# Opening of a two-layer transformer kernel: norms in halves, one load of the first input, kept projections in half pieces

## The chip, the cores and the metric

The kernel runs on one core of one Trainium2 chip. Its five engines are TensorE (PE), VectorE (DVE), ScalarE (ACT), GpSimd (POOL) and SyncE (SP). The metric is the device time of one execution in microseconds (us), taken as the median of several runs.

## What is computed

Four sequences (b = 0 to 3) of 1024 tokens with 256 features go through two layers. Each layer is an attention and a feed-forward part, and after each part the input is added and the row is normalised. Only the first attention is touched by the change:

```python
qkv = jnp.einsum('bsc,oc->bso', x, w_qkv).reshape(B, S, 3, H, D)   # H = 16 heads, D = 16
q = layer_norm(qkv[:, :, 0], q_gamma, q_beta)                      # over the 16 elements of a head
k = layer_norm(qkv[:, :, 1], k_gamma, k_beta)
v = qkv[:, :, 2]
q, k = apply_rope(q, k)
attn = softmax(einsum('bqhd,bkhd->bhqk', q * D ** -0.5, k))
out = einsum('bhqk,bkhd->bqhd', attn, v).reshape(B, S, C) @ w_proj.T + b_proj
x = layernorm(x + out)
# then: gated feed-forward with integer weights; causal attention with a geometric term (8 heads);
# a mixture of 16 experts, two per token, with capacity 512; each followed by add and layernorm
```

All tensors are float32, apart from the three integer weights of the gated feed-forward.

## The kernel before

The first attention works on groups of four heads: a sequence has four groups (G0 = 4), and n = 4 * b + g numbers them. The order of instructions on every engine is written out by hand. Each engine runs its own list in order and waits on semaphores where it needs another's result; SP's list holds nearly all DMA issues.

**Projections.** The three weights (q, k, v) lie side by side in `w0`, 768 columns. The columns of q and k are centred over each head first, so that the mean in the norm falls away and only a sum of squares is left. A projection is cut into pieces j = 0 to 3 of 256 tokens. For each, `load_xin` loads a 256 KB tile of the transposed input (tag "xin", two buffers), four matmuls of 128x256 fill one PSUM bank, and ScalarE copies it out. `project_qk(b, pr)` does q and k for eight heads (pr is 0 or 1), with the sums of squares (`squares`, `sums`) and the inverse roots (`roots`); for b = 0, pr = 0 the root is taken at the end by ScalarE's Sqrt and VectorE's reciprocal, otherwise by GpSimd's power, 16 columns at a time. `project_v(b)` writes into `va0`, the one tile of values. `bank(name, big)` gives either one of six score banks (tag "s") or the single bank "m", which transposes use too.

**Stashes.** The projections of b = 1 to 3 don't fit into SBUF beside their turn. `stash_qk(b, pr)` and `stash_v(b)` compute them during the first batch and store them to DRAM (`qk_d`, `ss_d`, `v_d`); `load_heads` and `load_v` read them back. Only the values of b = 1 aren't kept: `project_v(1)` runs between the first two batches. The stored tile `xs` has one buffer, so the next stash's first copy waits until the store has read it.

**Maxima and attention.** `Maxima` turns the normalised heads (`rotate`: six steps for each of q and k and each half of the tokens), transposes them into `qT` and `kT` (`turn`), and computes the score matrix once only for the row maxima: `head(i, h)` is a matmul into a score bank and a VectorE reduction (tile `part`). `close` places the maxima into the 17th row of the query tile, so that the second computation of the scores has them subtracted. `Attend` computes the scores again, transposed (`sc`), exponentiates them on ScalarE (`pe`) and multiplies with the values (`av`).

**Order.** The opening projects for the first group and rotates it. Then come 16 units of maxima alone, group 0's: four maxima matmuls and four reductions each, with a projection piece of `early` beside most of them. `first_units(b)` then yields 64 units for a sequence: four scores, four maxima of the group after, one `av` of the unit before (four matmuls). `weave(units, n, pieces, ...)` spreads a list of pieces over the units, one piece after a unit, and runs `later` work at each `tick`; its `side` list adds one step of preparation to each unit (loads of x, `empty_slots`, weight conversion `dequant`). `empty_slots` fills the expert buffers `disp_d` in DRAM from a tile of zeros in twelve DMAs of 520 KB. In the first batch the pieces are 32 stashed ones and the mid step `load_heads(1, 0)` at unit 30.

Of the kernel before, what the change touches and what calls it, by code (L numbers as in the profile page):

```python
# [35 lines left out]
def postln_layers_kernel(ctx: ExitStack, tc: tile.TileContext, a: dict, out: bass.AP):  # L36
# [74 lines left out]
    with ExitStack() as main:  # L111
# [41 lines left out]
        for c in range(2):  # L153
            nc.sync.dma_start(w0[:, c], a["w0qkv"][c * P : (c + 1) * P, :])
# [10 lines left out]
        wsum0 = act.tile([P, 32], F32, tag="hT", bufs=1, name="wsum0")  # L165
        for c in range(2):
            w3 = w0[:, c, 0 : 2 * C].rearrange("p (h d) -> p h d", h=32)
            nc.vector.tensor_reduce(wsum0, w3, AX.X, ALU.add)
            nc.vector.tensor_scalar_mul(wsum0, wsum0, -1.0 / D0)
            nc.vector.tensor_tensor(w3, w3, wsum0.unsqueeze(2).to_broadcast([P, 32, D0]), ALU.add)  # L170
# [31 lines left out]
        nc.vector.memset(tokk, 0.0)  # L202
        nc.vector.memset(tokk[:, :, :, 16:17], 1.0)
        va0 = fa.tile([P, TB, H0, 32], F32, name="va0")
        nc.vector.memset(va0[:, :, :, 16:32], 1.0)
        nm3 = act.tile([P, 4, 4, 32], BF16, name="nm3")
        nc.vector.memset(nm3, 0.0)
# [4 lines left out]
        def project_qk(b, pr, first=False):  # L212


            def piece(j, big):
                if j == 0:
                    heads[b, pr] = (
                        fa.tile([P, TB, 2, 8, D0], F32, tag="xr", bufs=1, name=f"xr_{b}_{pr}"),
                        fa.tile([P, TB, 2, 8], F32, tag="ss", bufs=1, name=f"ss_{b}_{pr}"),
                    )  # L220
                xr, ss = heads[b, pr]
                xin = load_xin(b, j, f"k{pr}")
                ps = bank(f"qk0_{b}_{pr}_{j}", big)
                for i in range(2):
                    for c in range(2):
                        nc.tensor.matmul(
                            ps[:, i * 256 : (i + 1) * 256],
                            xin[:, c, i * P : (i + 1) * P],
                            w0[:, c, pr * 256 : (pr + 1) * 256],
                            start=c == 0,  # L230
                            stop=c == 1,
                        )
                x = xr[:, 2 * j : 2 * j + 2].rearrange("p t s h d -> p (t s h d)")
                nc.scalar.copy(x, ps)
                part = ss[:, 2 * j : 2 * j + 2].rearrange("p t s h -> p (t s h)")

                def squares():
                    sq = act.tile([P, 512], F32, tag="q1", bufs=G1, name=f"sq0_{b}_{pr}_{j}")
                    nc.gpsimd.tensor_tensor(sq, x, x, ALU.mult)

                    def sums():
                        nc.vector.tensor_reduce(part, sq.rearrange("p (h d) -> p h d", d=D0), AX.X, ALU.add)

                    return sums

                def roots(k):
                    p = part[:, 16 * k : 16 * k + 16]
                    if k == 0:
                        nc.gpsimd.tensor_scalar(part, part, D0 * 1e-6, None, ALU.add)
                    nc.gpsimd.tensor_tensor(p, p, neg_half.to_broadcast([P, 16]), ALU.pow)  # L250

                if first:
                    squares()()
                    if j == 3:
                        flat = ss.rearrange("p t s h -> p (t s h)")
                        nc.vector.tensor_scalar_add(flat, flat, D0 * 1e-6)
                        nc.scalar.activation(flat, flat, AF.Sqrt)
                        nc.vector.reciprocal(flat, flat)
                else:

                    def start():
                        sums = squares()
                        later(1, sums)

                    later(1, start)
                    for k in range(2):
                        later(3 + k, lambda k=k: roots(k))

            return [lambda big, j=j: piece(j, big) for j in range(4)]

        def project_v(b):
            def piece(j, big):
                xin = load_xin(b, j, "v")
# [21 lines left out]

        def stash_qk(b, pr):
            kept = {}

            def piece(j, big):
                if j == 0:  # L300
                    kept["x"] = act.tile([P, TB * 256], F32, tag="va1", bufs=1, name=f"xs_{b}_{pr}")
                    kept["ss"] = act.tile([P, TB * 16], F32, tag="k1", bufs=G1, name=f"sss_{b}_{pr}")
                xin = load_xin(b, j, f"k{pr}")
                ps = bank(f"qk0_{b}_{pr}_{j}", big)
                for i in range(2):
                    for c in range(2):
                        nc.tensor.matmul(  # L307
                            ps[:, i * 256 : (i + 1) * 256],
                            xin[:, c, i * P : (i + 1) * P],
                            w0[:, c, pr * 256 : (pr + 1) * 256],  # L310
                            start=c == 0,
                            stop=c == 1,
                        )
                x = kept["x"][:, j * 512 : (j + 1) * 512]
                nc.scalar.copy(x, ps)
# [15 lines left out]
            return [lambda big, j=j: piece(j, big) for j in range(4)]  # L331

        def stash_v(b):
            def piece(j, big):
                xin = load_xin(b, j, "v")
                ps = bank(f"v0_{b}_{j}", big)
                for i in range(2):
                    for c in range(2):
                        nc.tensor.matmul(
                            ps[:, i * 256 : (i + 1) * 256],  # L340
                            xin[:, c, i * P : (i + 1) * P],
                            w0[:, c, 512:768],
                            start=c == 0,
                            stop=c == 1,
                        )
                x = act.tile([P, 512], F32, tag="nmT", bufs=2, name=f"vs_{b}_{j}")
                nc.scalar.copy(x, ps)
                later(1, lambda: nc.sync.dma_start(v_d[b][:, j * 512 : (j + 1) * 512], x))

            return [lambda big, j=j: piece(j, big) for j in range(4)]  # L350
# [29 lines left out]
        class Maxima:  # L380


            def __init__(self, b, g, engines):
# [6 lines left out]

                def rotate(s, u):
                    eng, to_tok = engines[s], (self.tok, tokk)[s]
# [6 lines left out]
                    z = fa.tile([P, 4, 4, D0], F32, tag="tmpz", bufs=1, name=f"z0_{b}_{g}_{s}_{u}")  # L399
# [14 lines left out]
                def steps():  # L414
                    for s, u in ((0, 0), (1, 0), (0, 1), (1, 1)):
# [607 lines left out]
        both_pool = (nc.gpsimd, nc.gpsimd)  # L1023

        def first_units(b):
# [3 lines left out]
            for g in range(G0):  # L1029
# [3 lines left out]
                for i in range(16):  # L1033
# [27 lines left out]
                    if i == 3 and n + 2 < G0 * B:  # L1061
                        nb, ng = divmod(n + 2, G0)
                        groups[n + 2] = Maxima(nb, ng, both_pool)
# [84 lines left out]
        straight(project_qk(0, 0, first=True))  # L1148
        groups[0] = Maxima(0, 0, (nc.gpsimd, nc.vector))
        groups[0].rotate()  # L1150
        for k in range(4):
            groups[0].turn(k // 2, k % 2, big=k % 2 == 0)
        groups[1] = Maxima(0, 1, both_pool)

        b0p = wp.tile([P, C], F32, name="b0p")
        nc.scalar.dma_start(b0p, a["b0p"].partition_broadcast(P))
        w0p = wp.tile([P, 2, C], F32, name="w0p")
        nc.scalar.dma_start(w0p, a["w0p"].rearrange("(c p) f -> p c f", p=P))
# [400 lines left out]
```

## Time and profile before

| what | value |
|---|---|
| median of 3 runs | 2500.72 us (2499.29 to 2504.57) |
| profiled execution, its own time | 2496.14 us |
| span of the profiled execution | 2494.4 us |
| mean granted TensorE clock | 0.959 |
| PE busy | 2330.1 us |
| DVE busy | 1387.3 us |
| ACT busy | 1014.6 us |
| POOL busy | 769.8 us |
| 0 to 34.6 us (to the first reduction of maxima) | PE 15.71, DVE 21.26, ACT 7.56, POOL 21.11 us busy |
| 34.6 to 91.8 us (maxima of group 0 alone) | PE 50.99, DVE 44.17, ACT 11.29, POOL 38.73 us busy |
| 87.3 to 410 us (first batch) | PE 314.42, DVE 192.57, ACT 177.65, POOL 119.89 us busy |
| 410 to 430 us (between the batches) | PE 13.92, DVE 2.78, ACT 4.79, POOL 5.83 us busy |

The profile is of one execution; its times are us from the first instruction. A busy time counts instructions at work, not those that wait, and issues of DMAs don't count. The span leaves out what lies around the instructions, so the execution's own time is a little longer. "A <- B" in brackets says what ended an engine's idle time.

### The profile page before, as it was taken

To read this page: it belongs to the slowest core of one execution; us is meant where nothing else is said; L and a number is where in the kernel's file an instruction comes from. 1 tells how busy PE (TensorE), PEld (TensorE's weight loads), DVE (VectorE), ACT (ScalarE), POOL (GpSimd) and SP (SyncE) were. 2 spreads that over 40 slices of the span, in tenths; PEclk is the share of its full clock that TensorE was granted. 3 is DMA by queue.
4 is the path that set the end of the run, shared out by engine and by line. 5 is a ranking of instruction groups with operands and counts; after the bars stand their busy time and mean duration, and the time that the engine had idled before them with its cause. 6 is when DMAs were issued, how large, how long until landed. Compare 5 with 4: busy or idle time off the path is not lost.

```text
span 2494.4 us, 36151 instructions
## 1 busy us (share of the span) xinstructions
PE 2330.1 (93%) x14004; PEld 1162.9 (47%) x14004; DVE 1387.3 (56%) x3233; ACT 1014.6 (41%) x1995; POOL 769.8 (31%) x1111
## 2 busy tenths in 40 slices
PE   6999999999999999999989999999999974999994
PEld 4343344444444454444445434445556432666662
DVE  6765554766656747687565567825645774111113
ACT  1455454555453345545523455463332331111112
POOL 5723622524123313454042321211112145212223
PEclk8999999999998999999989999999999886999997
DMA  3134223000000000001000000102000012444444
GB/s 96 31 108 134 73 66 101 1 27 1 1 1 27 1 1 1 24 24 54 24 8 1 1 1 1 46 23 99 1 1 1 1 48 73 102 103 118 104 89 145
DMA packets 79772, 109.87 MB, mean 44 GB/s; under 512 B 8944, under 2 KB 68592, under 8 KB 77936
## 3 DMA queue, kind: packets, MB, share of 16 engines
q1 hardware_dynamic: 54080, 80.21, 9.9%
q0 software_dynamic: 9984, 14.82, 3.1%
q10 hardware_dynamic: 15536, 12.53, 1.7%
q8 instruction: 110, 1.80, 0.3%
q14 instruction: 62, 0.51, 0.1%
HBM read 68.64 MB, written 38.90 MB: 43 GB/s over the span
## 4 chain that ended last, share of the span: by engine, by line
PE 85%; DVE 8%; POOL 3%; DMA 2%; issue 1%; ACT 1%; ACTq 0%; SPq 0%; DVEq 0%; POOLq 0%
PE sc L468 19%; PE av L486 10%; PE ph L1420 7%; PE gu L632 7%; PE py L1436 7%; PE sc L958 5%; PE mx L444 5%; PE mx L908 4%; PE p L877 4%; PE dn L648 3%; PE av L995 3%; PE dn L995 2%; DVE masked L918 2%; PE ppa L566 2%; PE qk L307 2%; PE pt L435 1%
## 5 line engine op out<-in xcount | busy, mean ns | idle before, releaser
L447 DVE TENSOR_REDUCE part<-mx 128x1 f32<-128x512 f32 x1024 | 656.3, 684 | 353.5 <-PE mx L444 347.4
L477 ACT ACTIVATE pe<-sc 128x512 f32<-128x512 f32 x1024 | 554.1, 596 | 392.8 <-PE mx L444 332.9
L444 PE MATMUL mx<-kT,qT 32*128 32x512 f32 x2048 | 654.1, 645 | 5.5 <-DVE part L447 5.2
L468 PE MATMUL sc<-qT,kT 32*128 32x512 f32 x2048 | 620.5, 637 | 0.3 <-ACT pe L477 0.3
L468 PEld LDWEIGHTS sc<-qT,kT 32*128 32x128 f32 x2048 | 184.1, 183 | 227.3 <-issue 180.2
L486 PE MATMUL av<-pe,va 128*32 128x512 f32 x2048 | 273.6, 606 | 0.0
L969 ACT ACTIVATE pe<-sc 128x512 f32<-128x512 f32 (+3 forms) x384 | 157.5, 497 | 205.7 <-PE sc L958 199.1
L444 PEld LDWEIGHTS mx<-kT,qT 32*128 32x128 f32 x2048 | 198.9, 186 | 56.1 <-DVE part L447 29.6
L918 DVE CUSTOM_DVE_ANT_0 masked<-mx,mask_w 128x128 bf16<-128x128 f32 (+3 forms) x256 | 125.4, 490 | 111.7 <-PE mx L908 80.5
L1420 PE MATMUL ph<-dmT,f 128*128 128x512 f32 x384 | 169.5, 600 | 4.4 <-DVE dmT L99 3.5
L1436 PE MATMUL py<-f,hTm 128*128 128x256 f32 x768 | 167.7, 379 | 0.0
L1428 ACT ACTIVATE hTm<-ph,b 128x512 f32<-128x512 f32 x96 | 60.7, 683 | 260.6 <-PE ph L1420 260.6
L972 POOL TENSOR_SCALAR_AFFINE_SELECT pe<-pe 128x256 f32<-128x256 f32 x128 | 54.1, 432 | 363.0 <-ACT pe L969 361.5
L1440 POOL DMA_INDIRECT acc_d<-yo,dm x48 | 74.7, 1556 | 284.0 <-DVE yo L1438 233.9
L1436 PEld LDWEIGHTS py<-f,hTm 128*128 128x128 f32 x768 | 146.1, 190 | 24.8 <-issue 5.7
L908 PE MATMUL mx<-kT,qT 32*128 32x512 f32 (+3 forms) x768 | 138.0, 577 | 4.7 <-DVE x L533 3.6
L365 POOL TENSOR_TENSOR ss<-ss,neg_half 128x16 f32<-128x16 f32 x48 | 139.1, 2906 | 0.5
L1437 DVE TENSOR_TENSOR yo<-py,b 128x256 f32<-128x256 f32 x48 | 20.4, 425 | 206.7 <-PE py L1436 206.7
L958 PE MATMUL sc<-qT,kT 32*128 32x512 f32 (+3 forms) x768 | 131.5, 569 | 4.0 <-DVE part L918 2.2
L486 PEld LDWEIGHTS av<-pe,va 128*32 128x32 f32 x2048 | 40.3, 108 | 192.9 <-issue 183.8
L1420 PEld LDWEIGHTS ph<-dmT,f 128*128 128x128 f32 x384 | 72.7, 192 | 94.2 <-issue 86.1
L632 PE MATMUL gu<-xTf,wg 128*128 128x256 f32 x384 | 107.2, 402 | 0.3 <-ACT pe L969 0.3
(340 smaller groups left out, 2969.7 us busy)
## 6 DMA issues: line engine op xcount, KB each, us to landing
f<-in_fc SPq DMA_DIRECT2D x14, 1024.0 KB, 5.0
f<-in_fc ACTq DMA_DIRECT2D x10, 1024.0 KB, 5.9
xink<-in_xT SPq DMA_DIRECT2D x32, 256.0 KB, 3.2
disp_d<-empty SPq DMA_DIRECT2D x12, 520.0 KB, 5.7
qk_d<-xs SPq DMA_DIRECT2D x6, 1024.0 KB, 4.0
xr<-qk_d SPq DMA_DIRECT2D x6, 1024.0 KB, 5.0
dm<-disp_d SPq DMA_DIRECT2D x11, 520.0 KB, 3.8
xinv<-in_xT SPq DMA_DIRECT2D x16, 256.0 KB, 4.1
```

Of the source, the lines that this page charges most:

```text
L444: nc.tensor.matmul(sc, self.qT[r, t * P : (t + 1) * P], self.kT[r, u * 512 : (u + 1) * 512], start=True, stop=True)
L447: return lambda: nc.vector.tensor_reduce(self.part[:, t, u, h : h + 1], sc, AX.X, ALU.max, negate=True)
L468: nc.tensor.matmul(sc, self.m.kT[r, kt * P : (kt + 1) * P], self.m.qT[r, qb * 512 : (qb + 1) * 512], start=True, stop=True)
L477: nc.scalar.activation(self.pes[i, h // 2][:, h % 2, :], sc, AF.Exp)
L486: nc.tensor.matmul(self.av[32 * h : 32 * h + 32, :], va0[:, kt, 4 * self.g + h, :], self.pes[i, h // 2][:, h % 2, :], start=kt == 0, stop= ...
L632: nc.tensor.matmul(ps[:, i * 256 : (i + 1) * 256], w[:, c, f * P : (f + 1) * P], xT[j][:, c, :], start=c == 0, stop=c == 1,)
L908: nc.tensor.matmul(scs[h][:, :n], qT[r, t * P : (t + 1) * P], kT[r, u * 512 : u * 512 + n], start=True, stop=True,)
L918: nc.vector.tensor_tensor_reduce(masked[:, :n], scs[h][:, :n], mask_w[:, 512 - n :], -1.0, -NEG, ALU.add, ALU.min, part)
L958: nc.tensor.matmul(scs[h][:, off:], ones_h[r, :] if w else kT[r, kt * P : (kt + 1) * P], (self.m.nmT if w else qT)[r, q], start=w == 0, st ...
L969: nc.scalar.activation(pe[:, j, off:], scs[2 * hp + j][:, off:], AF.Exp)
L1420: nc.tensor.matmul(ph[:, i * CAP : (i + 1) * CAP], f1[:, c, (f + i) * P : (f + i + 1) * P], dmT[:, c, :], start=c == 0, stop=c == 1,)
L1436: nc.tensor.matmul(py[:, :C], hT[:, f, c * P : (c + 1) * P], f2[:, f, :], start=f == 0, stop=f == FF1 // P - 1)
```

## The change

The first input is loaded once, into four tiles `xin0` (the buffers that later hold `pe`), and all three projections of b = 0 read them. The weights come in three slices of columns, and `centre(pr)` centres each half of the q and k columns by itself. Squares are taken by ScalarE out of PSUM instead of by GpSimd, and the first projection's roots are taken for each half of the tokens; the second projection's are taken all at once by Sqrt and reciprocal too. Several memsets go from VectorE to GpSimd. `Maxima` takes an engine for each (q or k, half); the key's first half is rotated by VectorE, the rest by GpSimd, and VectorE's rotation has its own tile for z. `project_v(0)` runs before the first maxima, ahead of the two transposes that they need; the other two follow inside the units, whose order is 0, 2, 4, 6, 1, 3, 5, 7, 8 to 15. Stashed projections are cut in two: a half piece is two matmuls and a copy of 256 columns. Twelve half pieces of `stash_v(2)` and `stash_v(3)` run beside the first maxima, the remaining 52 halves in the first batch. `project_v(1)` is woven into the second batch. The weight loads go from ScalarE's queue to SP's, the twelve `disp_d` stores from SP's to ScalarE's.

```diff
-        for c in range(2):
-            nc.sync.dma_start(w0[:, c], a["w0qkv"][c * P : (c + 1) * P, :])
+        xin0 = [act.tile([P, 2, 256], F32, tag="pe", bufs=4, name=f"xin0_{j}") for j in range(4)]
...
+        nc.sync.dma_start(w0[:, :, 0:256], w0_in[:, :, 0:256])
+        load_xin0(0)
+        load_xin0(1)
+        nc.sync.dma_start(w0[:, :, 256:512], w0_in[:, :, 256:512])
+        load_xin0(2)
+        load_xin0(3)
+        nc.sync.dma_start(w0[:, :, 512:768], w0_in[:, :, 512:768])
...
+        nc.scalar.activation(spacer, neg_half, AF.Sqrt, scale=-1.0)
...
+        def centre(pr):
+            w4 = w0[:, :, pr * 256 : (pr + 1) * 256].rearrange("p c (h d) -> p c h d", h=16)
...
+        centre(0)
...
-        nc.vector.memset(tokk, 0.0)
-        nc.vector.memset(tokk[:, :, :, 16:17], 1.0)
+        nc.gpsimd.memset(tokk, 0.0)
+        nc.gpsimd.memset(tokk[:, :, :, 16:17], 1.0)
...
-        nc.vector.memset(va0[:, :, :, 16:32], 1.0)
+        nc.gpsimd.memset(va0[:, :, :, 16:32], 1.0)
...
+            def roots(lo, hi):
+                r = flat[:, lo:hi]
+                nc.vector.tensor_scalar_add(r, r, D0 * 1e-6)
+                nc.scalar.activation(r, r, AF.Sqrt)
+                nc.vector.reciprocal(r, r)
...
+                nc.scalar.activation(sq, ps, AF.Square)
+                nc.scalar.copy(xr[:, 2 * j : 2 * j + 2].rearrange("p t s h d -> p (t s h d)"), ps)
...
+                if pr:
+                    later(1, sums)
                     if j == 3:
+                        later(2, lambda: roots(0, 128))
                 else:
+                    sums()
+                    if j % 2:
+                        roots(j // 2 * 64, j // 2 * 64 + 64)
...
-                xin = load_xin(b, j, "v")
+                xin = load_xin(b, j, "v") if b else xin0[j]
...
+        def half(ps, xin, i, cols):
+            for c in range(2):
+                nc.tensor.matmul(
+                    ps[:, 0:256], xin[:, c, i * P : (i + 1) * P], w0[:, c, cols], start=c == 0, stop=c == 1
+                )
...
+                if i == 0:
+                    kept["in"] = load_xin(b, j, f"k{pr}")
+                ps = bank(f"qk0_{b}_{pr}_{j}_{i}", big)
+                half(ps, kept["in"], i, slice(pr * 256, (pr + 1) * 256))
                 x = kept["x"][:, j * 512 : (j + 1) * 512]
-                nc.scalar.copy(x, ps)
+                nc.scalar.copy(x[:, i * 256 : (i + 1) * 256], ps[:, 0:256])
+                if i == 0:
+                    return
...
+                half(ps, kept["in"], i, slice(512, 768))
+                x = kept["x"]
+                nc.scalar.copy(x[:, i * 256 : (i + 1) * 256], ps[:, 0:256])
+                if i == 1:
+                    later(1, lambda: nc.sync.dma_start(v_d[b][:, j * 512 : (j + 1) * 512], x))
...
-                    z = fa.tile([P, 4, 4, D0], F32, tag="tmpz", bufs=1, name=f"z0_{b}_{g}_{s}_{u}")
+                    pool, tag = (fa, "tmpz") if eng is nc.gpsimd else (act, "sg")
+                    z = pool.tile([P, 4, 4, D0], F32, tag=tag, bufs=1, name=f"z0_{b}_{g}_{s}_{u}")
...
-        straight(project_qk(0, 0, first=True))
-        groups[0] = Maxima(0, 0, (nc.gpsimd, nc.vector))
+        straight(project_qk(0))
+        groups[0] = Maxima(
+            0, 0, {(0, 0): nc.gpsimd, (1, 0): nc.vector, (1, 1): nc.gpsimd, (0, 1): nc.gpsimd}
+        )
         groups[0].rotate()
-        for k in range(4):
-            groups[0].turn(k // 2, k % 2, big=k % 2 == 0)
-        groups[1] = Maxima(0, 1, both_pool)
+        centre(1)
+        values0 = project_v(0)
+        for k in range(3):
+            values0[k](k != 2)
+        groups[0].turn(0, 0, big=True)
+        groups[0].turn(1, 0, big=True)
+        values0[3](False)
+        groups[1] = Maxima(0, 1)
...
-        nc.scalar.dma_start(b0p, a["b0p"].partition_broadcast(P))
+        nc.sync.dma_start(b0p, a["b0p"].partition_broadcast(P))
...
-                nc.sync.dma_start(to, empty["z"])
+                nc.scalar.dma_start(to, empty["z"])
...
-        early = project_v(0) + project_qk(0, 1)
-        for i in range(16):
+        stash = []
+        for b in range(1, B):
+            stash += stash_qk(b, 0) + stash_qk(b, 1)
+        early = stash_v(2) + stash_v(3)
+        second = []
+
+        for k, i in enumerate((0, 2, 4, 6, 1, 3, 5, 7, *range(8, 16))):
             for red in [groups[0].head(i, h) for h in range(4)]:
                 red()
             tick()
-            groups[1].rotate(5)
-            if i == 8:
+            groups[1].rotate(4)
+            if k == 2:
+                groups[0].turn(1, 1, name="l")
+            if k == 5:
+                groups[0].turn(0, 1, name="l")
+            if k == 8:
                 groups[0].close(0)
-            if i == 10:
+                second = project_qk(1)
+            if k == 10:
                 groups[0].turn(0, 0, name="a")
-            elif 12 <= i:
-                groups[1].turn((i - 12) // 2, i % 2)
-            elif early and i != 4:
+            if k >= 12:
+                groups[1].turn((k - 12) // 2, k % 2, big=True)
+            if 8 <= k < 12:
+                second.pop(0)(True)
+            else:
                 early.pop(0)(False)
...
         weave(
-            first_units(0), 64, [wait, wait] + stash, False, [lambda big: load_heads(1, 0)], 30, [f for f in prep if f], 0
+            first_units(0), 64, early + stash, False, [lambda big: load_heads(1, 0)], 30, [f for f in prep if f], 0
         )
         flush()
-        straight(project_v(1))
         load_heads(1, 1)
         for t in range(TB):
             load_x(1, t)
-        weave(first_units(1), 64, first_end(0) + ffn0(0) + project1(0), False, [lambda big: load_heads(2, 0)], 30)
+        weave(first_units(1), 64, project_v(1) + first_end(0) + ffn0(0) + project1(0), False, [lambda big: load_heads(2, 0)], 30)
```

## Prediction

> **What bounds the kernel now.** I read the page's engine shares and its chain first, since they say whose time is the span.
>
> ```profile
> PE 2330.1 (93%) x14004; PEld 1162.9 (47%) x14004; DVE 1387.3 (56%) x3233; ACT 1014.6 (41%) x1995; POOL 769.8 (31%) x1111
> ...
> PE 85%; DVE 8%; POOL 3%; DMA 2%; issue 1%; ACT 1%; ACTq 0%; SPq 0%; DVEq 0%; POOLq 0%
> ```
>
> TensorE carries 85% of the chain, so away from the opening only its work or its waiting counts. Next the timeline of the opening.
>
> ```profile
> 7.59 5.71 PE L226 MATMUL qk<-w,xink 128*128 128x256 f32 x16 [7.59 <-DMA xink<-in_xT]
> ...
> 17.59 1.22 DVE L242 TENSOR_REDUCE ss<-sq 128x32 f32<-128x512 f32 x2
> ...
> 34.62 2.48 DVE L447 TENSOR_REDUCE part<-mx 128x1 f32<-128x512 f32 x4 [3.66 <-PE mx L444]
> ```
>
> Projection starts at 7.59, the sums at 17.59, the first maxima at 34.62. The chain of waits over the 16 units of maxima alone (up to about 91.8) shows what those wait for.
>
> ```profile
> 35.57 4.80 DMA dirs<-in_dirs
> 40.37 0.58 ACT va L284
> ...
> 63.68 2.92 POOL ss L250
> ...
> 70.84 2.93 POOL ss L250
> ...
> 78.81 1.05 PE pt L435 x4
> ```
>
> ScalarE is held by its own weight DMAs, and later GpSimd's powers (line 250) stand on the chain. Then TensorE's timeline in two units of the first attention batch, the first with a stash piece, the second without.
>
> ```profile
> 108.97 1.07 PE L486 MATMUL av<-pe,va 128*32 128x512 f32 x8
> ...
> 111.04 1.99 PE L307 MATMUL qk<-w,xink 128*128 128x256 f32 x8
> ...
> 114.03 1.06 PE L486 MATMUL av<-pe,va 128*32 128x512 f32 x8
> ...
> 118.03 1.07 PE L486 MATMUL av<-pe,va 128*32 128x512 f32 x8
> ```
>
> From one av to the next: 5.06 with the piece, 4.00 without. A piece takes 1.92 of TensorE but lengthens its unit by 1.07: an empty unit waits about 0.86 for score banks to be emptied, and a piece fills that. Last, the chain at the seam between the batches, where project_v(1) stands alone:
>
> ```profile
> 412.04 3.15 DMA xinv<-in_xT
> 415.33 6.65 PE v L277 x16
> 421.99 2.67 DMA xinv<-in_xT
> 424.79 1.97 PE v L277 x8
> ```
>
> [...] SP issued the wd_i load at 284.35, when GpSimd had converted wu, and the xink load behind it at 284.82; TensorE got that input 5.16 us later. [...] four transposes took 1.11 after a pause and 0.66 in steady work. [...]
>
> **Opening, to the first maxima.** The first 256 columns of w0 (256 KB) are loaded alone. Before, 384 KB landed at 4.59 and the next 384 KB at 6.47, so 256 KB takes 1.25 and lands near 4.0 (estimate). Centring them is 0.69 + 0.18 + 0.69, so TensorE starts near 5.8. Four pieces, the first cold (7.59 to 11.3 before, 3.7) and three at 2.0, end near 15.5; the one load per input removes the buffer wait at 14.19. The rope tables stay in VectorE's way until 14.0, because gam lands at 8.4. The memsets behind them (0.91 + 0.09 + 1.76 + 0.27 = 3.0) move to GpSimd, which idled 7.2 there: free; without that idle, 3.0. Squares move from GpSimd (1.04) to ScalarE, no row here; I take a copy's 0.58. They queue ahead of the copies, and the first root waits with two squares and two copies behind it (2.4), so the second half's roots end near 19.5 (22.7 before). VectorE's key rotation took 3.2: 22.7. But TensorE now has three value pieces (6.0) before the transposes: 21.5. Transposes, copies and the fourth value piece bring the first maxima to about 26.2 against 34.62: **-8.4**, bounds -4 and -11.
>
> **Sixteen units of maxima.** Before, 34.6 to 91.8: 57.2. VectorE's floor is 16 x 2.48 = 39.7, four sums at 0.69, one root (add, Sqrt, reciprocal: 1.55 at 21.16) and close 0.18: 44.2. The twelve weight DMAs leave ScalarE (7.7 of issue) for SP, idle between 17 and 25. GpSimd's eight powers of 2.9 go. TensorE has 1.07 + 0.96 per unit with a half piece, below 2.48; with a full one, 3.0, in only four units, below 3.17 with its sum. What is added: stash_v's store on SP waits for ScalarE's copy, and the next xinv load queues behind it, 0.35 + 3.2 before it lands. TensorE waits about 2.2, VectorE 1.5 after using up its banks; four times: 6. So 50.2: **-7**, bounds 0 and -12.
>
> **First attention batch.** From av to av, 92.17 to 409.05, 316.9 for 62 units. 62 x 3.99 = 247.4; 30 transposes at 0.59 (4.58 against 3.99) = 17.7; 31 pieces at 1.07 = 33.2; the remaining 18.6 are waits: 7.1 behind wd_i, 4.6 behind a store of sums at 383, 3.4 for an xinv behind a store at 188, the rest small. After: twelve halves are gone to the opening and 51 lie in these units. TensorE's sum with a half is 1.00 + 1.07 + 0.96 + 1.07 = 4.10, so 0.11 each, 5.6. No row shows a half: four transposes at this place cost 0.00 (unit of 4.00 at 434.87), the low end; 0.5 is the high end[...]. Waits: wd_i still stands behind GpSimd, whose casts and powers need about 45 from the first wg cast, while ten shortened units need 42; with 5 for landing, less a unit of grace: 4. At five seams between stashes the copy into xs comes one unit after the last, but the 1 MB store takes 4.0: 5 x 1.2. Loads behind the store of sums 3 x 0.5; twelve disp_d issues on ScalarE (0.5 each, mostly in its idle 1.5 per unit; exps are queued behind them, and banks wait for those) 12 x 0.2; others 2: together 16, bounds 8 and 32. Sum 286.7: **-30**, bounds -38 and +6.
>
> **Seam.** Project_v(1) held TensorE from 410.6 to 426.8: 16.2. Woven in, its four pieces fill units: 4 x 1.07 = 4.3. But its first load now queues on SP behind the stash store, 1 MB of xr and eight x loads, whose last waits for xr: issue took 6.1 (423.39 to 429.45). I put xinv 14.5 after the seam, one unit of 4 covers part: 10.5. **-1.4**, bounds -9 and +5. The later stages keep their orders: 0; a changed clock could give or cost a microsecond.
>
> **Sum.** -8.4 - 7 - 30 - 1.4 = -46.8: the profiled execution, 2496.1 (span 2494.4), becomes 2449.3. The median of the runs is 2500.7, 4.6 above; from it, 2453.9, so **2454**.
>
> **Rivals.** 0.2% is 5 us, about what a measurement can tell from no change.
> 1. Halves are not free: 0.5 each, 51 x 0.5 = 25.5 instead of 5.6, so -27, 2474. For it: the one m bank also serves the transposes. Against: a piece beside a transpose cost 5.65 = 3.99 + 0.59 + 1.07, nothing extra.
> 2. An insertion has one price, whatever its size: 51 x 1.07 = 54.6, +49 on the forecast, 2503: no change. Against: the free transposes at 434.87.
> 3. Slower: late inputs. 26 input loads lie in the first batch. If SP, in order behind stores, lets every one cost its landing of 3.2, that is 83 instead of 16: 2521. It decides from (46.8 + 16) / 26 = 2.4 each. For it: the waits at 188, 284 and 383. Against: q/k loads run two buffers ahead, some four units of 4.1, over 3.2.
> 4. The opening doesn't shorten, because gam and the value pieces hold it and VectorE waits for loads: +13, 2467.
>
> **How the numbers follow.** The forecast 0.62, rival 1 0.16, rival 2 0.05, rival 3 0.07, rival 4 0.10. The likeliest case's own range is 2440 to 2468. To leave no more than 2 in 10 outside, and with bounds as wide as the waits', I take 2436 to 2484; rivals 2 and 3 lie outside. Faster 0.88, same 0.05, slower 0.07.
>
> **What would show it.** First maxima near 26; no powers on the chain before the first scores; the first scores near 72; av to av about 4.1 with a half; a TensorE wait of some 10 for xinv in the second batch's first unit. Periods near 5 with a half would refute the main step; DMA waits above 60 in the first batch would make it slower.

## The result, and the profile after

The median of four runs is 2486.13 us (2485.72 to 2493.76) where the kernel before, in its own four runs, has 2501.90 (2499.29 to 2504.57): a ratio of 0.9947, 95% interval 0.9933 to 0.9960. The changed kernel is faster by 15.8 us; the forecast was 2454, and its range ended at 2484. A second comparison, with five runs of the changed kernel, gave 0.9955 (0.9943 to 0.9968). The profiled execution of the changed kernel took 2493.76 us (span 2492.0), the longest of its runs, so the stages below are read from three profiles of each kernel, not from one.

The page of the changed kernel, first its engine shares and then the shares of its chain:

```profile
PE 2331.3 (94%) x14004; PEld 1156.8 (46%) x14004; DVE 1384.9 (56%) x3227; ACT 1020.2 (41%) x2037; POOL 743.9 (30%) x1101
...
PE 86%; DVE 7%; DMA 3%; POOL 2%; issue 1%; ACT 1%; SPq 0%; DVEq 0%; ACTq 0%; POOLq 0%
```

TensorE has the same 14004 instructions, so it was its waiting that could change. DMA's share of the chain has gone up from 2% to 3%, a first sign that something now waits for loads or stores; it doesn't say where. The opening, from the timeline (start, duration, engine and line; in brackets the idle time before and what ended it):

```profile
6.54 8.84 PE L249 MATMUL qk<-w,xin 128*128 128x256 f32 x32 [6.54 <-DVE w L186]
...
12.63 1.27 DVE L261 TENSOR_REDUCE ss<-sq 128x32 f32<-128x512 f32 x2
...
25.65 1.88 DVE L453 TENSOR_REDUCE part<-mx 128x1 f32<-128x512 f32 x3 [1.76 <-PE mx L450]
```

Projection starts at 6.54, the first maxima are reduced at 25.65 instead of 34.62. One unit of the first attention batch with a half piece, from TensorE's timeline:

```profile
97.44 1.06 PE L492 MATMUL av<-pe,va 128*32 128x512 f32 x8
...
99.50 1.13 PE L303 MATMUL v<-w,xinv 128*128 128x256 f32 x4
...
101.63 1.07 PE L492 MATMUL av<-pe,va 128*32 128x512 f32 x8
```

From av to av it is 4.19, so a half lengthens its unit by 0.20. By stage, in us, the middle of three profiles of each kernel:

| stage | before | after | difference | forecast |
|---|---|---|---|---|
| up to the first reduction of maxima | 34.62 | 25.65 | -9.0 | -8.4 |
| sixteen units of maxima, to the first av | 57.55 | 67.59 | +10.0 | -7 |
| first batch, first to last av | 315.79 | 290.08 | -25.7 | -30 |
| seam and second batch, to its last av | 349.76 | 352.50 | +2.7 | -1.4 |
| on to the last av of the fourth batch | 943.46 | 944.25 | +0.8 | 0 |
| last stretch, to the end | 796.25 | 807.68 | +11.4 | 0 |
| sum | | | -9.8 | -46.8 |

The sum agrees with the second comparison (11 us) better than with the first (16). Two rows miss by over 10: the maxima and the last stretch. For the maxima, the waits of the stage (engine and what it waited for: us in total, times, longest):

```profile
ACT vs L349 <- PE v L303: 33.3, 11, 6.3
DVE part L453 <- PE mx L450: 23.5, 11, 5.8
...
PE v L303 <- DMA xinv<-in_xT: 13.2, 4, 4.4
```

VectorE, which should set the pace there, waits 23.5 for scores, and TensorE, which makes them, waits four times for an input. The timeline shows two of the four:

```profile
29.61 0.33 SPq L351 DMA_DIRECT2D v_d<-vs  x1
...
29.98 0.43 SPq L148 DMA_DIRECT2D xinv<-in_xT  x1
...
33.27 1.50 PE L303 MATMUL v<-w,xinv 128*128 128x256 f32 x4 [2.18 <-DMA xinv<-in_xT]
...
78.03 0.33 SPq L351 DMA_DIRECT2D v_d<-vs  x1
...
78.45 0.39 SPq L148 DMA_DIRECT2D xinv<-in_xT  x1
...
82.26 2.05 PE L303 MATMUL v<-w,xinv 128*128 128x256 f32 x4 [4.38 <-DMA xinv<-in_xT]
...
84.23 2.09 PE L450 MATMUL mx<-kT,qT 32*128 32x512 f32 x8
...
86.34 2.48 DVE L453 TENSOR_REDUCE part<-mx 128x1 f32<-128x512 f32 x4 [5.77 <-PE mx L450]
```

SP issues the store of the tile that ScalarE has just copied, and the load of the next tile right behind it; the tile is used 3.3 to 3.8 later, and TensorE has nothing else. In the second case the copy itself was late, since ScalarE had stood 3.77 at the root ahead of it. After three of the four pauses TensorE ("the array") has a granted clock of 0.50 for a while: 3.4 us after the pause of 2.18, 6.8 after those of 3.51 and 4.38, none after that of 3.18. At half clock the half piece takes 2.05 instead of 1.13, the scores 2.09 instead of 1.14; below, "cold" stands for this. One such wait kept VectorE idle for 5.77.

At the seam SP's queue has the same form (SP's issues and the first value piece, from the timeline):

```profile
383.96 0.34 SPq L330 DMA_DIRECT2D qk_d<-xs  x1
...
385.80 0.34 SPq L331 DMA_DIRECT2D ss_d<-sss  x1
...
387.35 5.77 SPq L525 DMA_DIRECT2D x<-in_x  x8
...
393.25 7.43 SPq L148 DMA_DIRECT2D xinv<-in_xT  x3
...
396.50 3.78 PE L282 MATMUL v<-w,xinv 128*128 128x256 f32 x8 [8.78 <-DMA xinv<-in_xT]
```

The input of project_v(1) stands behind the stash store, the store of the sums and eight x loads; TensorE waits 8.78, and the piece takes 3.78, cold (the granted clock is 0.50 from 388.8 to 402.5), instead of 1.99.

### The profile page after: what moved, and what is told of

Same layout as the page of the kernel before. It is cut to its first block, busy times and chain, and to the rows that moved or that the text cites. A ratio compares the mean times of both kernels' runs of the same rounds, so it can differ in the third digit from the quotient of the medians.

```text
span 2492.0 us, 36155 instructions
## 1 busy us (share of the span) xinstructions
PE 2331.3 (94%) x14004; PEld 1156.8 (46%) x14004; DVE 1384.9 (56%) x3227; ACT 1020.2 (41%) x2037; POOL 743.9 (30%) x1101
## 4 chain that ended last, share of the span: by engine, by line
PE 86%; DVE 7%; DMA 3%; POOL 2%; issue 1%; ACT 1%; SPq 0%; DVEq 0%; ACTq 0%; POOLq 0%
PE sc L474 19%; PE av L492 10%; PE ph L1439 7%; PE gu L638 7%; PE py L1455 7%; PE sc L964 5%; PE mx L914 4%; PE mx L450 4%; PE p L883 4%; PE dn L654 4%; PE av L1001 3%; PE dn L1001 2%; PE ppa L572 2%; DVE masked L924 2%; PE qk L303 2%; PE pt L441 1%
## 5 line engine op out<-in xcount | busy, mean ns | idle before, releaser
L450 PE MATMUL mx<-kT,qT 32*128 32x512 f32 x2048 | 631.4, 646 | 2.1 <-DVE part L453 1.9
L474 PE MATMUL sc<-qT,kT 32*128 32x512 f32 x2048 | 606.4, 639 | 0.0
L474 PEld LDWEIGHTS sc<-qT,kT 32*128 32x128 f32 x2048 | 176.4, 183 | 220.3 <-issue 178.4
L450 PEld LDWEIGHTS mx<-kT,qT 32*128 32x128 f32 x2048 | 188.2, 185 | 40.0 <-DVE part L453 18.6
```

Source lines behind the costliest of these rows:

```text
L450: nc.tensor.matmul(sc, self.qT[r, t * P : (t + 1) * P], self.kT[r, u * 512 : (u + 1) * 512], start=True, stop=True)
L474: nc.tensor.matmul(sc, self.m.kT[r, kt * P : (kt + 1) * P], self.m.qT[r, qb * 512 : (qb + 1) * 512], start=True, stop=True)
```

## The experiments

All are edits of the changed kernel unless said otherwise; each ratio refers to runs of the kernel before that were taken beside the edited one. The changed kernel was timed in the same comparison as the early loads of stash_v, the early loads of project_v(1) and the whole pieces; where the others are set against its median, that is across comparisons, in which the medians of the kernel before lie 1 to 2 us apart. "Early" below means ahead of the stores in SP's queue. The theory at the start: the maxima stage gave back what the opening won because each load stands behind a store, and the seam loses about 9 in the same way.

### The changed kernel again

> The changed kernel once more, to stand beside the others: about 15 us below the kernel before (ratio near 0.994). First reduction of maxima at 25.7, first av at 93, sixty-third av at 380, as in its first profile. If the 4.4 us that the first second_units stage lost there are an accident of how long the clock stays halved after its pause, they differ in this profile; if they belong to the change, they return.

2486.26 us, ratio 0.9955 (0.9943 to 0.9968). First reduction 25.44, maxima stage 65.55, first batch 290.08: as in the first profile, within 2.1. The second batch's end to the third's first av took 165.84 (166.85 in the first profile, 162.45 in the first profile of before). The kernel before, profiled again, settles that row:

> The kernel before once more, for a second profile. If the later stages differ between the two kernels only because halved clock stretches fall by accident, this profile shows the second_units stages at other than 162.5 and 166.3 or the last stretch at other than 796, nearer to the changed kernel's 165.8, 168.2 and 808. If the change lengthens them, they return as they were.

There it is 167.35, so the 4.4 us which that stage seemed to lose were an accident of one profile. The last stretch came back at 798.72, near its 796.25.

### Loads one tile ahead in stash_v

```
 if i == 0:
-    kept["in"] = load_xin(b, j, "v")
+    if j == 0:
+        kept[0] = load_xin(b, 0, "v")
+    if j < 3:
+        kept[j + 1] = load_xin(b, j + 1, "v")
+    kept["in"] = kept[j]
```

> stash_v loads tile j+1 one piece early, ahead of the store of tile j in SP's queue; nothing else is changed. Theory (the loads behind the stores cost the maxima stage its gain, TensorE going cold in each wait): the sixteen units fall from 67.6 to 52 to 56, first av near 79, total 11 to 15 us below the changed kernel. Rival (the halves and the transposes put into the stage lengthen it, or VectorE does): the stage stays above 64, total within 3 us of the changed kernel.

2467.50 us, ratio 0.9884 (0.9870 to 0.9899), 18.8 below the changed kernel in the same comparison and more than the 11 to 15 expected. First av at 75.85: the stage took 49.76. Its waits, for the one line shown above as 23.5:

```profile
DVE part L457 <- PE mx L454: 5.9, 7, 1.6
```

VectorE's wait fell by 17.6, the stage by 17.8. TensorE over the stage, the changed kernel first and then this one (stretch, length and busy time, instructions, granted clock, DMA share, GB/s):

```profile
25.65:93.24 67.59, 53.67 (x253) 0.87 0.17 49
```

```profile
26.09:75.85 49.76, 48.24 (x252) 1.00 0.21 68
```

For the same work the array was busy 5.4 less: with the pauses the half clock went too, and the mean granted clock rose from 0.87 to 1.00. The rival, that halves and transposes lengthen the stage, falls: they are all still there.

### The store on another queue

```
-later(1, lambda: nc.sync.dma_start(v_d[b][:, j * 512 : (j + 1) * 512], x))
+later(1, lambda: nc.scalar.dma_start(v_d[b][:, j * 512 : (j + 1) * 512], x))
```

> stash_v's store goes out on ScalarE's queue instead of SP's; nothing else is changed. Theory (the place of the store ahead of the load costs the maxima stage 16 to 18): SP now runs ahead with the loads, so as e1, the stage at 49 to 53 and the total 14 to 19 below the changed kernel. Rival (it was loading a piece early that helped, through something other than the store): under 6 below.

2463.35 us, ratio 0.9851 (0.9825 to 0.9876). The stage again took 49.76. Two different edits, which share only that the load no longer stands behind the store, give the same stage to 0.01: this is shown. The total, 22.9 below the changed kernel, is more than expected because its last stretch took 797.5 where the changed kernel has 806 to 810; up to the last av of the second batch the gain is 17.5 to 20.8.

### The seam, two ways

Early loads for project_v(1):

```
+ahead_v = {j: load_xin(1, j, "v") for j in range(2)}
 flush()
 load_heads(1, 1)
...
-weave(first_units(1), 64, project_v(1) + first_end(0) + ...
+weave(first_units(1), 64, project_v(1, ahead_v) + first_end(0) + ...
```

> The first two inputs of project_v(1) are loaded ahead of the last stash store, the heads and the eight x loads; nothing else is changed. Theory (at the seam TensorE waits 9 us for an input queued behind them, then runs cold): the stretch from the sixty-third av to the last av of the second batch falls by 8 to 10, total 7 to 10 us below the changed kernel. Rival (the pieces woven in are what costs, up to 1.9 each and one unit with two pieces more): 0 to 3 below.

2480.43 us (2472.43 to 2480.92), ratio 0.9927 (0.9913 to 0.9942), 5.8 below the changed kernel. The timeline at the seam:

```profile
379.97 0.37 SPq L148 DMA_DIRECT2D xinv<-in_xT  x1
...
380.39 0.46 SPq L330 DMA_DIRECT2D qk_d<-xs  x1
...
384.07 2.00 PE L282 MATMUL v<-w,xinv 128*128 128x256 f32 x8
...
384.31 5.79 SPq L525 DMA_DIRECT2D x<-in_x  x8
```

From the last av of the first batch to the first of the second it is 7.20, where the changed kernel's three profiles have 17.50 to 18.78; the second batch is the same 334.58. So the wait cost 10.3 to 11.6 and this removes all of it, as the theory has it; the total shows a little less than expected, within the spread of its runs. The other way, back to the straight run:

```
 flush()
+straight(project_v(1))
 load_heads(1, 1)
...
-weave(first_units(1), 64, project_v(1) + first_end(0) + ...
+weave(first_units(1), 64, first_end(0) + ...
```

> project_v(1) runs straight at the seam again, as before the change; nothing else is changed. Theory (woven in, its pieces cost 5.4 in the second batch and its first input 9 of waiting, together what the straight run of 16 cost): within 3 us of the changed kernel, the seam back at about 21.8 and the second batch at 329.2. Rival (weaving it in is a gain by itself, as the forecast's seam step has it, or a loss by itself of 6): 5 or more to one side.

2481.28 us, ratio 0.9935 (0.9922 to 0.9948), 5 below the changed kernel by the medians. The seam is 20.30 and the second batch 329.18, together 349.5 against 352.5. Weaving the pieces in, as the change does it, is a loss of about 3 by the stage, as the theory has it; the 5 of the medians, across comparisons, lies at the border of the rival. With its input early it is a gain of 7.7 (341.8).

### Whole pieces in place of the halves

stash_qk, and in the same way the last two tiles of stash_v, as before the change; the twelve half pieces among the maxima stay.

```
-half(ps, kept["in"], i, slice(pr * 256, (pr + 1) * 256))
+full(ps, kept["in"], slice(pr * 256, (pr + 1) * 256))
 x = kept["x"][:, j * 512 : (j + 1) * 512]
-nc.scalar.copy(x[:, i * 256 : (i + 1) * 256], ps[:, 0:256])
+nc.scalar.copy(x, ps)
...
-return [lambda big, j=j, i=i: piece(j, i, big) for j in range(4) for i in range(2)]
+return [lambda big, j=j: piece(j, 0, big) for j in range(4)]
```

> The twelve half pieces of the opening stay; the 26 whole pieces that are left run whole in the first batch, in place of 51 halves. Theory (whole pieces cost 1.07 each, halves 0.20): 26 x 1.07 - 51 x 0.20 = 17.6, with 0 to 7 us of waits more: 17 to 25 us above the changed kernel, so about as long as the kernel before or up to 10 longer. Rival (the first batch gained by its waits and by having fewer pieces in it, not by their size): under 8 above the changed kernel.

2503.55 us, ratio 1.0023 (1.0016 to 1.0030), 17.3 above the changed kernel. The first batch took 306.08 instead of 290.08: 16.0 longer, for 17.6 worked out from 1.07 and 0.20. With the new opening and seam in place, the halves carry more than the whole gain of the change; without them it would be slightly slower than the kernel before.

### Both early loads

The edit of stash_v and the first edit of the seam, together.

> Both early loads together: stash_v loads one tile ahead, and the first two inputs of project_v(1) are loaded before the last stash store. Theory (two separate waits of the same kind, at two places): the gains add, 19 of the first and 6 to 10 of the second, total near 2459 where the changed kernel has 2486, ratio to the kernel before 0.984 to 0.986. Rival (the time moves to another wait or is lost to a lower clock later): under 22 us below the changed kernel.

2460.86 us, ratio 0.9856 (0.9839 to 0.9872), 25.4 below the changed kernel. Maxima 49.77, seam 7.20: the two add.

### One root in place of two

```
-if j % 2:
-    roots(j // 2 * 64, j // 2 * 64 + 64)
+if j == 3:
+    roots(0, 128)
```

> One root over all 64 tokens rows x 128 sums after the fourth piece, in place of two over half of them; nothing else is changed. Theory (VectorE's key rotation begins only after both roots anyway, TensorE has three value pieces to do before the transposes): first reduction of maxima at 25 to 27, as with halves at 25.4. Rival (GpSimd's query rotation waits for the roots, and the transposes for it): 2.8 later, 28 or more.

(What is meant is one root over all 128 sums that a partition holds.) First reduction at 26.02, where the three profiles with halves have 25.44 to 25.70. In the trace GpSimd's query rotation did wait 2.99 for the roots, but the query transposes, at 21.41 instead of 20.39, still were done before the key transposes, at 22.54 instead of 22.18, which wait for VectorE. By the trace the halves of the norms are worth 0.4 us at most; the first reduction alone can't tell this from nothing, since with the same opening and whole pieces in the first batch it came at 26.32.

### The first input loaded for each projection

```
-xin0 = [act.tile([P, 2, 256], F32, tag="pe", bufs=4, name=f"xin0_{j}") for j in range(4)]
...
+xin0 = {}
...
+xin0[0, 0] = load_xin(0, 0, "k0")
+xin0[0, 1] = load_xin(0, 1, "k0")
...
+x0 = xin0.get((pr, j)) or load_xin(0, j, f"k{pr}")
...
-xin = load_xin(b, j, "v") if b else xin0[j]
+xin = load_xin(b, j, "v")
```

> The first input is loaded anew for each of its three projections, through the two buffers of xin, in place of one load into four buffers; nothing else is changed. The forecast's opening step rests on the one load removing the buffer wait. If so: third and fourth piece wait for their loads, first reduction of maxima 3 to 6 later than 25.4, total 3 to 12 above the changed kernel (the second q/k projection then also loads, among the maxima). Rival (loads are ahead anyway): within 1.5 at the first reduction, total within 3.

2489.97 us, ratio 0.9953 (0.9934 to 0.9971), 3.7 above the changed kernel by the medians. That hides most of it, since the last stretch took 797.7 here: first reduction at 28.68, 3.0 later, as expected, and the maxima stage 79.88, some 12 more. Its waits:

```profile
DVE part L449 <- PE mx L446: 37.0, 12, 7.0
...
PE v L299 <- DMA xinv<-in_xT: 18.0, 5, 5.4
...
PE qk L245 <- DMA xink<-in_xT: 3.0, 1, 3.0
```

Five waits of the stash in place of four, and one more for the second q/k projection. The single load matters, less for the opening than for the stage behind it.

### Half pieces alone, on the kernel before

An edit of the kernel before: half, stash_qk and stash_v as in the change, and

```
-weave(first_units(0), 64, [wait, wait] + stash, False, ...
+weave(first_units(0), 64, stash, False, ...
```

> The kernel before with the kept pieces of its first attention batch cut in halves and the two empty steps ahead of them dropped; opening and seam are as before. Theory (half pieces by themselves carry the gain of the change: 31 x 1.07 - 62 x 0.20 = 20.8): 16 to 22 below the kernel before, ratio 0.991 to 0.9935. Rival (the gain needed fewer pieces in the batch): under 10 below. And on the last 800 us: if it lasts about 797 as in both profiles of before, the new opening or the seam makes it 808 in the changed kernel; if 807 or more, the half pieces do or it is an accident of the clock.

2509.64 us (2496.62 to 2518.74), ratio 1.0027 (1.0013 to 1.0042): slower, by its last stretch of 807.5, since it ends its second batch at 759.91, where the kernel before has 755.29 to 760.07. The theory as I had it falls. The rival is nearer, but says nothing of why the halves don't pay here. The first batch took 316.11, for 316.88, 315.79 and 315.56 in the three profiles of before. The units without a wait have the expected 4.20 and 4.78, but TensorE's waits in the batch (the last shown line is ScalarE's, from the timeline) are:

```profile
PE v L298 <- DMA xinv<-in_xT: 11.8, 7, 3.3
PE qk L298 <- DMA xink<-in_xT: 4.9, 2, 2.9
PE sc L466 <- ACT pe L475: 3.7, 1, 3.7
```

```profile
263.98 0.37 ACT L314 COPY xs<-qk 128x256 f32<-128x256 f32 x1 [5.77 <-DMA qk_d<-xs]
```

With whole pieces in every second unit a store goes out in the unit between, and the load behind it has a unit's time to land. With a half in every unit that free unit is gone: the next tile is wanted one unit after the store. A unit with a half is 4.20, and in the kernel before such a load lands 3.2 (q/k) or 4.1 (values) after its issue, by the medians. In the changed kernel six of the eight tiles of stash_v have left this batch for the maxima stage, and took those waits with them. The last line is the seam between two stashes: ScalarE stood 5.77 at a copy into xs until the 1 MB store had read it, with the exponentials queued behind it.

If that is right, the halves must pay on the kernel before as soon as the loads are early. The edit: one list of all kept tiles, and

```
+def xin_ahead(b, j, name):
+    n = line.index((b, name, j))
+    for m in range(n, min(n + 2, len(line))):
+        if m not in got:
+            bb, nn, jj = line[m]
+            got[m] = load_xin(bb, jj, nn)
+    return got[n]
...
-kept["in"] = load_xin(b, j, "v")
+kept["in"] = xin_ahead(b, j, "v")
```

and the same in stash_qk.

> The kernel before with half pieces, and the kept inputs loaded one tile ahead of their use; opening and seam as before. Theory (halves cost 0.20 each in the first batch, and what made the halves alone worthless was inputs queued behind stores): first batch 281.7 us plus waits of 5 to 15, so 287 to 297 for 316.9 before and 316.1 with halves alone; total 15 to 28 below the kernel before. Rival (halves only pay where there are fewer pieces): batch above 305, total within 8 of the kernel before.

2475.19 us, ratio 0.9909 (0.9893 to 0.9926). The batch took 291.99, 24 less than before, and TensorE's waits in it:

```profile
PE sc L480 <- ACT pe L489: 3.6, 1, 3.6
PE qk L298 <- ACT xs L328: 0.5, 1, 0.5
```

No input is waited for. One unit of 11.72, at a copy into xs between two stashes as above, stays. The price of 0.20 was right; what made the halves worthless alone was the place of the loads. With the old opening and the old seam, this kernel ends its second batch at 734.46, as early as the changed one (733.57 to 736.89); that its median is 11 lower is the last stretch, of which more below.

### All kept inputs and project_v(1) from one list

The same xin_ahead in the changed kernel, its list ended by the four tiles of project_v(1):

```
-xin = load_xin(b, j, "v") if b else xin0[j]
+xin = xin_ahead(b, j, "v") if b else xin0[j]
...
+xin_ahead(1, 0, "v")
 flush()
```

> All the kept pieces and project_v(1) load their inputs from one list, one tile ahead of their use, so ahead of the stores. Theory: beyond the 25 of both early loads together it removes the waits for inputs in the first attention batch (four, 0.9 to 1.8 long, lengthening their units by 1 to 2 each): 4 to 7 below that kernel, about 2455 where the changed kernel has 2486. Rival (the units' ends are set by the copies and not by the inputs there): within 2 of 2460.

2444.41 us (2443.08 to 2452.36), ratio 0.9774 (0.9750 to 0.9798): the fastest here, 55 us below the kernel before. The first batch took 281.98, 4.9 less than with both early loads, as expected. Most of the rest of the 16 between the two medians is the last stretch, 796.9 against 807.0.

### The last stretch

The last 800 us hold the same instructions in all these kernels, and yet differ by 10 us. Three more profiles:

> The changed kernel a third time, for the time of its last stretch (after the last av of the fourth batch). An accident of the execution: 797 or 808 with no rule, so 797 here would show it. A property of the changed kernel: 807 to 811 again.

> The kernel before a third time, for the same stretch. An accident: 807 or more may come here. A property of the kernel before: 796 to 799 again.

> The version with all inputs one tile ahead a second time, for the same stretch, which was 797 in its first profile. An accident: 807 or more may come here. A property of the kernel: 797 again. The stretch up to the last av of the second batch is to return at 699.

The changed kernel: 810.39, 807.68 and now 806.05. The kernel before: 796.25, 798.72, 795.35. The one-list version: 796.94, 797.38, and its second batch ended at 700.16. In these profiles, then, a kernel keeps its value. Runs without a profile don't always: of the one-list version's six runs one took 2452.36 at a mean granted clock of 0.957, the others 2443.08 to 2445.43 at 0.962 to 0.964; of the five with early loads for project_v(1) one took 2472.43 at 0.956, the others 2477.71 to 2480.92 at 0.952. And the value follows no edit that I made: of the other kernels seven (both early loads, each of the seam's two, the early loads of stash_v, whole pieces, one root, halves on the kernel before) have 806.5 to 810.8, and three (store on ScalarE, input loaded anew, halves with early loads on the kernel before) 795.9 to 797.7. Their difference is in the granted clock: its mean over the stretch is 0.93 in the first profile of before, and 0.90 to 0.91 in the first two of the changed kernel and in those of the early loads of stash_v, the early loads of project_v(1) and the whole pieces. After the same pause of 3.41 us for ptm<-ident_h,nm at its start, TensorE's windows of the kernel before and of the changed kernel (its second profile), columns as above:

```profile
1714.90:1721.80 6.90, 6.68 (x29) 0.51 0.27 114
```

```profile
1692.30:1709.30 17.00, 16.37 (x57) 0.50 0.26 104
```

Half clock for 6.8 and for 17.0; in the third profile of before it is 6.8 again, in the first and third of the changed kernel 17.1. That is 3.9 of the 11 us: up to the end of the next such pause, of 3.35 us, the kernel before takes 202.3 and the changed kernel 206.0 to 206.2. But the one-list version takes 206.2 there too and is short all the same. What divides nine profiles, six short (the first and third of before, store on ScalarE, halves with early loads, both of the one-list version) and three long (the first and third of the changed kernel, halves on the kernel before), is the work behind this second pause. Up to the end of TensorE's next wait of 2.2 us for mx it takes 93.6 to 97.8 at a mean granted clock of 0.88 or 0.95 in the six, 104.6 to 105.7 at 0.78 to 0.79 in the three. And this goes with the moment at which the clock is halved: 0.7 to 0.9 or 1.6 us after the second pause has ended in the six, 1.2 and 1.5 after it in two of the three, 1.4 ahead of it in the last (halves on the kernel before). The changes of the clock lie on a grid of 3.41 us in these nine (see below), so where the pause lies between two points of that grid seems to decide. No run moved that pause alone; that it decides, and why, is not shown.

## Why the prediction was right or wrong, step by step

**Opening, -8.4: right, at -9.0.** TensorE started at 6.54 (forecast 5.8), the second roots ended at 18.5 (19.5), the first maxima came at 25.65 (26.2). One part of it had the wrong weight: the norms in halves, worth 0.4 at most by the experiment.

**Sixteen units of maxima, -7: wrong, at +10.0.** This is the step that failed: 67.59 for a forecast of 50.2. The forecast saw the mechanism, the load behind the store, but put too little on it: four waits at 2.2 for TensorE and 1.5 for VectorE, 6 in all. Measured: 2.2 to 4.4 for TensorE, 13.2 in all, and 17.8 for the stage (17.6 of VectorE's waiting), shown by what vanished with the early loads. Two things were left out. After three of the four pauses the array was cold, at a granted clock of 0.50 for 3.4 to 6.8 us, so that the piece behind it took up to 2.05 for 1.13 and the scores 2.09 for 1.14, though the forecast itself had read four transposes at 1.11 after a pause and at 0.66 in steady work. And 0.35 + 3.2 - 2.2 leaves TensorE 1.3 of work after the load's issue; it had 1.1 in the first case, 0.3 and 0.2 in the next two and none in the last, where it stood idle before the load was issued. Those waits account for 11.8 of the miss of 17.4. The other 5.6 lie in the rest of the sum: without the waits the stage is 49.76, where the forecast had VectorE's 44.2. VectorE is busy 45.00 there, close to that, but still waits 5.9 for scores, in seven waits of at most 1.6, while TensorE is busy 48.24. The forecast priced TensorE by the unit and found it below VectorE; no run takes these short waits apart. The first scores of attention, forecast near 72, came at 88.8, and at 71.4 with the early loads.

**First batch, -30: nearly right, at -25.7.** A half costs 0.20, not 0.11: 51 x 0.09 = 4.6, the whole miss. It lies well below rival 1's 0.5, an estimate for which no row stood, which is out. The text counted 62 periods where there are 63; one unit of 4.0 therefore sits in its waits, 18.6 before and 16 after, on both sides. With 63 the waits are 14.6 and about 11, so the size of that term held. What the forecast did not see is why it held: the tiles whose stores cause such waits had moved into the maxima.

**Seam, -1.4: +2.7.** The late input was put at 10.5 and cost 10.3 to 11.6: right. The term that was short is that of the four pieces woven in: about 7 in place of 4.3. With its input early the seam is 7.20, 1.6 above the 21.83 - 16.2 = 5.6 left of it without the straight run, and the second batch is 5.4 longer, half of that in its last unit, which now holds two project1 pieces (7.31 for 4.57 before).

**Later stages, 0: +0.8 up to the fourth batch, then +11.4.** "A changed clock could give or cost a microsecond" was too small by ten. With the same instructions and, at the start of the last stretch, the same two pauses, this was not to be read from the profile of before; it is a term for the range.

**Rivals.** Rival 3, late inputs, named the mechanism but put it in the first batch, where inputs cost 5.5 in the changed kernel; the cost fell on the stage in front and on the seam. Rival 4 is out by the first reduction at 25.65; of its +13, only the opening's 8.4 was worked out. Rival 2 is out by 0.20 against 1.07.

**Queue and clock.** SP issued the store at 78.03, when ScalarE's copy had ended at 78.01, and the load only then, at 78.45, and two edits of what stands ahead of the loads in SP's queue gave 17.8. In the nine profiles named under the last stretch, every change of the granted clock ahead of the record's end lies within 0.1 us of a grid of 3.41 us, whose offset differs from one execution to the next (1.45 and 1.92 us in the first and third profile of before, 3.11 and 0.86 in those of the changed kernel). The forecast had no term for how long the half clock lasts; after one pause it lasted for 14 us of work (last section).

## What to carry to other kernels

In a queue in which stores and loads are issued in order, a load belongs ahead of the store of the tile before it; one tile ahead was worth 17.8 us here in one stage, and decided whether cutting pieces in two gained 24 us or nothing. When work is cut finer or packed denser, ask what its empty slots were hiding: here each gave a load the time to land. A wait of TensorE costs its length and, after three of the four here, the cold clock behind it (0.50 for 3.4 to 6.8 us), so price both.

## What the runs showed of the hardware that I had not expected

In the first profiles of the kernel before and of the changed kernel the half-clock stretches last whole multiples of 3.41 us: 3.4, 6.8, 10.2, 13.7, 17.1, 20.5, 37.5 and 41.0; only the last, 34.0 and 33.4, which runs to the end of the record, does not. At one and the same place, a pause ahead of the third stage of attention (ptm<-ident_h,nm), the stretch lasted 13.7 in the first profile of before, 17.1 in the third, 20.5 in the first of the changed kernel and 17.1 in its third. The pause was 3.9, 4.3, 3.9 and 4.8 us long. In the first three of these the half clock began 3.4, 1.2 and 2.5 us ahead of it, while the profile shows TensorE busy, so there the pause isn't its whole cause. In that first profile of the changed kernel TensorE had been busy again, without a gap worth naming, for 14 us before the full clock came back. Among the maxima a pause of 3.18 left the clock full and one of 2.18 was followed by half clock. So the time for which a pause is paid isn't read from its length; over the last stretch the kernels, at the same work, differ by some 10 us, with a mean granted clock of 0.93 in the short first profile of before and of 0.90 to 0.91 in the long ones that are given above.
